# The second layer's last stage of a graph-attention kernel: corrections by ScalarE and DMA, block products in another order

## The chip, the cores and the metric

The kernel runs on one core of a Trainium2 chip. The core has TensorE (PE, with its weight loads as PEld), VectorE (DVE), ScalarE (ACT), GpSimd (POOL) and SyncE (SP). Each engine works through a queue of its own in order, and semaphores tie the queues together. Transfers are issued from SP, ACT or POOL and run on 16 shared DMA engines. The metric is the device time of one execution in microseconds; lower is better.

## The reference

Two layers of graph attention on 512 nodes with 768 features, with 16,896 edges, a residual and a layer norm:

```python
def gat_layer(x, W, a_s, a_d, b, edge_index, concat):
    h = (x @ W).reshape(n, H, C)
    alpha_s = jnp.einsum('nhc,hc->nh', h, a_s)
    alpha_d = jnp.einsum('nhc,hc->nh', h, a_d)
    e = jax.nn.leaky_relu(alpha_s[src] + alpha_d[dst], NEG_SLOPE)
    m = jax.ops.segment_max(e, dst, num_segments=n)
    e = jnp.exp(e - m[dst])
    denom = jax.ops.segment_sum(e, dst, num_segments=n)
    alpha = e / (denom[dst] + EPS)
    out = jax.ops.segment_sum(h[src] * alpha[:, :, None], dst, num_segments=n)
    ...
    return out + b
h = gat_layer(x, W1, a_src1, a_dst1, b1, edge_index, concat=True)    # 8 heads of 768
h = jax.nn.elu(h)
out = gat_layer(h, W2, a_src2, a_dst2, b2, edge_index, concat=True)  # 1 head of 768
x = _layernorm(x + out, axis=-1)
```

## The kernel before

All matrices are float32. The edge list becomes a 512 x 512 matrix of counts, so that the softmax over edges is a dense softmax over rows, and the sum over edges is a dense product. Nodes are held in four tiles of 128 rows, t = 0 to 3, features in six chunks of 128. For each of the 8 heads the kernel projects x, makes the softmax, aggregates and multiplies into the second layer's input h2. Products are made from blocks with fewer multiplications than usual: seven block products (named P1 to P7) take the place of eight, and sums of blocks before and after make up for it.

What each engine does in which order is written out by hand: `run(script, ops)` goes through a string of names and calls the operation behind each. The engines wait for each other by semaphores that follow from the tiles read and written. The last script is `END`. It holds the last head's aggregation (names such as P10), its product with the second weight matrix (m.P1.0 with the eviction e.P1.0), the second layer's softmax (2lift, 2leak, 2rank, 2den, 2part, 2in), and the last stage, which the change is about: the second layer's aggregation, the residual and the layer norm.

In that last stage PT holds the four quadrants of the transposed, unnormalized attention matrix. `2in3` is the last of four copies on ACT (L906) that put the transposed tiles into PT. Sums of quadrants are made on DVE: a0 to a3 on the attention side (L1316, L1317), c0 to c3 on the feature side (L1318, L1319). `f.P6.0` is the block product P6 for the first of two tiles of a half (`final`, two matmuls of 384 columns in the program, four in the trace). Each takes a PSUM bank as accumulator: A for P1 and P2, B for a copy of P1 with P6, P7 and P4 added, F for P5 and P3. `f.fork0` is the copy from bank A into bank B on ACT (`fork_`, L1336); P2 may add to A only after it.

The output is xr + rden * (accumulated products), where xr holds x + b2, row tile by row tile, in an SBUF tile (named hs in the trace, as is the output tile), and rden is the inverse of the softmax denominators. The evictions on DVE are named by quadrant and half: y11 (rows 0 and 1, left 384 columns), y21 (rows 2 and 3, left), y22 (rows 2 and 3, right), y12 (rows 0 and 1, right). They are made by `result` (L1347), which also starts the row's statistics (L1353). The right half needs bank B at two earlier moments as well: after P6 (`xu0`, `xu1` for rows 0 and 1) and after P7 (`xw0`, `xw1` for rows 2 and 3). There `less_` (L1340) computes B * rden - xr into xr on DVE, and the later evictions subtract xr. P7 may add to B only after xu has read it, P4 only after xw, and P3 may add to F only after y22.

At a row's end come the aggregate of its statistics and a square root on ACT (`all`, L1359, L1361), the reciprocal and the offset (`inv`, L1366, L1368), a scaling of the row on ACT and a transfer to the output (`whole`). The row that comes last, row 3, is finished in two halves, on ACT and on DVE (`right3`, `left3`), and its last eviction is cut into pieces of 256 and 128 columns (y21.1a, y21.1b).

Of the kernel before, what the change touches and what calls it, by code (L numbers as in the profile page):

```python
# [8 lines left out]
F32 = mybir.dt.float32  # L9
# [4 lines left out]
AF = mybir.ActivationFunctionType  # L14
ALU = mybir.AluOpType
# [22 lines left out]
def gat_pass(  # L38
# [29 lines left out]
    L, R = slice(0, HALF), slice(HALF, D)  # L68
# [7 lines left out]
    small = ctx.enter_context(tc.tile_pool(name="small", bufs=4))  # L76
# [51 lines left out]
    W1, W2, A, kept_tiles = {}, {}, {}, {}  # L128
# [24 lines left out]
    TH = 2 * P  # L153
# [127 lines left out]
    for j in range(2):  # L281
        nc.vector.tensor_reduce(picks[:, j:j + 1], ident.rearrange("p (j k) -> p k j", k=32)[:, j, :], axis=AX.X,
                                op=ALU.add)
# [30 lines left out]
    else:  # L314
# [808 lines left out]
    def fold(parts):  # L1123
# [22 lines left out]
        """m.P12 lift2 lift3 F2 e.P12 g.P13 m.P1 e.P1 g.P11 m.P0 leak2 e.P0 m.P13 g.P10 rank2 out1 m.P10 e.P13 g.P6 e.P10 in0  # L1146
        m.P4 leak3 rank3 e.P4 m.P11 seed g.P8 w.P3 out2 m.P6 e.P11 g.P3 e.P6 g.P14 m.P8 w.P7 m.P14 e.P14 g.P5 m.P3 out3 l1
        in1 e.P3 m.P7 m.P5 e.P7 l2 l3 e.P5 e.P8"""]
    END = """in2 P10 fork0 ls0 in3 P11 fork1 P20 ls1 P21 P12 n0 nn0 n1 fork2 N0 nn1 r0 P22 n2 nn2 r1 P50 N2 P60 u0 r2 P61 P70 u1
        w0 r3 N1 x0 P71 P40 w1 b0 P30 y0 ls2 B0 vadd P62 P51 u2 P41 x1 b1 P72 w2 P31 y1 B1 P42 f0 P52 f1 F0 x2 m.P1.0 ls3 ld2  # L1150
        b2 B2 P32 e.P1.0 m.P1.1 ld0 y2 F1 f2 ld1 m.P2.0 F2 ld3 e.P1.1 g.0 m.P2.1 rows0 w.0 g.1 rows1 row2 g.3 e.P2.1 m.P6.0
        e.P2.0 spread m.P6.1 own g.2 2lift1 e.P6.0 m.P7.0 m.P7.1 2lift0 w.1 2leak0 2leak1 e.P7.0 2lift2 2rank1 2lift3 fold2
        2leak2 2rank0 m.P4.0 e.P7.1 2rank2 2leak3 2part0 2den0 2den1 m.P4.1 2rank3 fold0 2part1 e.P4.0 e.P4.1 2part2 2in0
        m.P5.0 2part3 e.P6.1 m.P5.1 2den3 fold4 e.P5.0 2den2 2in1 fold1 m.P3.0 e.P5.1 m.P3.1 2in2 e.P3.0 2in3 f.P1.0 f.fork0
        f.P1.1 fold5 fold3 e.P3.1 c0 a0 f.P2.0 c1 a1 a2 y11.0 f.fork1 f.P2.1 c2 y11.1 f.P5.0 f.P6.0 xu0 c3 f.P6.1 xu1 f.P7.0
        a3 xw0 f.P7.1 y22.0 xw1 f.P5.1 f.P3.0 y22.1 f.P3.1 y12.0 f.P4.0 all0 f.P4.1a y12.1 inv0 all1 f.P4.1b whole0 y21.0
        all2 inv1 inv2 y21.1a whole1 whole2 hint y21.1b all3 inv3 right3 left3"""
# [93 lines left out]
    xr = load_x()  # L1251
# [71 lines left out]
    def final(p, i, name, cols=L):  # L1323
        def f():
            start = (name, i) not in bank
            if start:
                bank[name, i] = mm.next()
            for k in range(2):
                nc.tensor.matmul(bank[name, i][:, cols], A2[p][:, k, i * P:(i + 1) * P], C2[p][:, k, cols],  # L1329
                                 start=start and k == 0, stop=k == 1, skip_group_check=True)  # L1330
        return f

    def fork_(i):
        def f():
            bank["B", i] = mm.next()
            nc.scalar.copy(bank["B", i][:, :HALF], bank["A", i][:, :HALF])  # L1336
        return f

    def less_(i, t, cols):
        return lambda: nc.vector.scalar_tensor_tensor(xr[:, t, cols], bank["B", i][:, :HALF], rden[t], xr[:, t, cols],  # L1340
                                                      op0=ALU.mult, op1=ALU.subtract)

    def result(name, i, t, cols, op, free, place=None):
        def f():
            if y[0] is None:
                y[0] = hpool.tile([P, NT, D], F32, name="hs")
            nc.vector.scalar_tensor_tensor(y[0][:, t, cols], bank[name, i][:, cols if cols != R else L], rden[t],  # L1347
                                           xr[:, t, cols], op0=ALU.mult, op1=op)
# [4 lines left out]
            nc.vector.bn_stats(stats[t][:, (0 if cols == L else 1) if place is None else place, :], y[0][:, t, cols])  # L1353
        return f

    def whole_row(t):
        def f():
            mv[t] = small.tile([P, nc.vector.BN_AGGR_DIM], F32, name="mv")
            nc.vector.bn_aggr(mv[t], stats[t])  # L1359
            rstd[t] = small.tile([P, 1], F32, name="rstd")  # L1360
            nc.scalar.activation(rstd[t], mv[t][:, 1:2], AF.Sqrt, bias=eps_ln)  # L1361
        return f

    def inverse(t):
        def f():
            nc.vector.reciprocal(rstd[t], rstd[t])  # L1366
            off[t] = small.tile([P, 1], F32, name="off")
            nc.vector.scalar_tensor_tensor(off[t], mv[t][:, 0:1], -1.0, rstd[t], op0=ALU.mult, op1=ALU.mult)  # L1368
        return f

    def right_out(t):
        def f():
            nc.scalar.activation(y[0][:, t, R], y[0][:, t, R], AF.Identity, bias=off[t], scale=rstd[t])
            nc.scalar.dma_start(out[t * P:(t + 1) * P, R], y[0][:, t, R])
        return f

    def left_out(t):
        def f():
            nc.vector.tensor_scalar(y[0][:, t, L], y[0][:, t, L], mv[t][:, 0:1], rstd[t], op0=ALU.subtract, op1=ALU.mult)
            nc.sync.dma_start(out[t * P:(t + 1) * P, L], y[0][:, t, L])  # L1380
        return f

    for i in range(2):
        for p, name in (("P1", "A"), ("P2", "A"), ("P6", "B"), ("P7", "B"), ("P4", "B"), ("P5", "F"), ("P3", "F")):
            ops[f"f.{p}.{i}"] = final(p, i, name)
        ops.update({f"f.fork{i}": fork_(i), f"xu{i}": less_(i, i, R), f"xw{i}": less_(i, 2 + i, R),
                    f"y11.{i}": result("A", i, i, L, ALU.add, True), f"y21.{i}": result("B", i, 2 + i, L, ALU.add, True),
                    f"y22.{i}": result("F", i, 2 + i, R, ALU.subtract, False),
                    f"y12.{i}": result("F", i, i, R, ALU.subtract, True)})
    def row_out_whole(t):  # L1390
        def f():
            nc.scalar.activation(y[0][:, t, :], y[0][:, t, :], AF.Identity, bias=off[t], scale=rstd[t])
            nc.sync.dma_start(out[t * P:(t + 1) * P, :], y[0][:, t, :])
        return f

    wide_part, last_part = slice(0, TH), slice(TH, HALF)
    for n, part_, place in (("a", wide_part, 0), ("b", last_part, 2)):
        ops[f"f.P4.1{n}"] = final("P4", 1, "B", part_)
        ops[f"y21.1{n}"] = result("B", 1, 3, part_, ALU.add, False, place)
    for t in range(NT):  # L1400
        ops.update({f"all{t}": whole_row(t), f"inv{t}": inverse(t)})
        if t + 1 < NT:
            ops[f"whole{t}"] = row_out_whole(t)
    ops.update(right3=right_out(3), left3=left_out(3))

    def hint():
        if not general:
# [33 lines left out]
```

## Time and profile before

| | us |
|---|---|
| median of 3 runs (616.43 to 617.2) | 616.57 |
| the profiled execution | 617.08 |
| its span | 615.3 |
| PE busy in it | 603.7 (98%) |
| DVE busy | 518.4 (84%) |
| ACT busy | 303.9 (49%) |
| POOL busy | 90.5 (15%) |
| last stage, from the first block product to the last aggregate | 588.28 to 609.16 |

The span runs from the first to the last record of the profiled execution; launch and end lie outside it. Times in the views count from the start of the span. Busy time of PE comes from modelled ends, so a busy PE is not a PE at its peak. The chain of waits follows the last instruction back, at each step to what released it. In the timeline a row gives start, duration, engine, line and tile names, and in brackets how long the engine had been idle before and what released it. A row can stand for several instructions (x4).

### The profile page before, as it was taken

What the parts mean: (1) busy time and instruction counts of PE and PEld (TensorE: products, weight loads), DVE (VectorE), ACT (ScalarE), POOL (GpSimd) and SP (SyncE); (2) the same over time, 40 slices, a digit from 0 to 9 for tenths busy, and PEclk for the clock granted to TensorE, in tenths of its full rate; (3) what the DMA queues carried; (4) which work ended last, traced back from release to release, by engine and by line L of the source; (5) the groups of instructions that cost most, each with busy time, mean ns of one, the idle gap of its engine ahead of it and who ended that gap; (6) DMA issues with size and microseconds to landing.
All of it is one profiled execution on the core that took longest, in us unless ns stands there. A gap on an engine that the chain in (4) does not pass through costs nothing.

```text
span 615.3 us, 8250 instructions
## 1 busy us (share of the span) xinstructions
PE 603.7 (98%) x2777; PEld 487.3 (79%) x2777; DVE 518.4 (84%) x1027; ACT 303.9 (49%) x556; POOL 90.5 (15%) x130
## 2 busy tenths in 40 slices
PE   8999999999999999999999999999999999999994
PEld 5665676688888888888888888888888888886652
DVE  6979967989997789878997789968996799868886
ACT  3118765623746166433746066432746056654643
POOL 1210103031300302022300303022200301020000
PEclk9999999999999999999999999999999999999998
DMA  8973898895947959295956959196875949290122
GB/s 290 312 160 95 242 248 226 224 278 81 342 77 230 214 176 243 52 337 79 334 98 198 234 160 271 37 325 104 292 143 157 271 96 275 42 215 2 32 38 106
DMA packets 95277, 112.85 MB, mean 183 GB/s; under 512 B 42822, under 2 KB 76158, under 8 KB 94334
## 3 DMA queue, kind: packets, MB, share of 16 engines
q1 hardware_dynamic: 74814, 89.06, 46.0%
q0 software_dynamic: 19984, 22.61, 23.1%
q10 hardware_dynamic: 432, 0.59, 0.3%
q8 instruction: 24, 0.39, 0.2%
q14 instruction: 23, 0.19, 0.1%
HBM read 98.73 MB, written 2.90 MB: 165 GB/s over the span
## 4 chain that ended last, share of the span: by engine, by line
PE 96%; DMA 2%; DVE 1%; ACT 1%; issue 0%; SPq 0%; ACTq 0%
PE mm L547 25%; PE mm L470 25%; PE mm L969 23%; PE mm L411 15%; PE mm L1329 2%; DMA hs<-in_x_dram 2%; PE tr L411 1%; PE bc L778 1%; PE mm L655 1%; PE tr L969 1%; DVE st L1353 0%; DVE hs L1347 0%; PE tr L1265 0%; PE mm L298 0%; PE tr L1329 0%; PE bc L1286 0%
## 5 line engine op out<-in xcount | busy, mean ns | idle before, releaser
L476 ACT ACTIVATE hs<-mm 128x512 f32<-128x512 f32 x36 | 21.5, 597 | 113.7 <-PE mm L470 111.1
L478 DVE TENSOR_TENSOR hs<-hs,mm 128x512 f32<-128x512 f32 x54 | 37.1, 687 | 39.9 <-PE mm L470 28.3
L969 PE MATMUL mm<-PT,hs 128*128 128x256 f32 x280 | 66.4, 380 | 1.0 <-ACT mm L975 0.5
L555 DVE TENSOR_TENSOR h<-h,mm 128x512 f32<-128x512 f32 x84 | 57.2, 682 | 7.5 <-PE mm L547 6.6
L969 PEld LDWEIGHTS mm<-PT,hs 128*128 128x128 f32 x280 | 52.8, 190 | 9.1 <-ACT mm L975 1.1
L547 PE MATMUL mm<-w1r,gT 128*128 128x256 f32 x240 | 54.8, 379 | 0.0
L547 PEld LDWEIGHTS mm<-w1r,gT 128*128 128x128 f32 x240 | 45.5, 190 | 6.4 <-DVE h L555 0.2
L187 POOL DMA_DIRECT2D w2t<-in_L_gnn_W_dram x18 | 24.7, 1682 | 143.8 <-DVE h L555 139.6
L470 PE MATMUL mm<-w2r,xT 128*128 128x256 f32 x192 | 44.5, 379 | 0.0
L470 PE MATMUL mm<-w2r,gT 128*128 128x256 f32 x192 | 44.4, 379 | 0.0
L898 ACT ACTIVATE q<-q,rden 128x512 f32<-128x512 f32 x28 | 20.2, 720 | 46.1 <-DVE rden L882 45.8
L906 ACT COPY PT<-zr 128x1024 uint16<-128x1024 uint16 x35 | 40.5, 1158 | 2.7 <-DMA zr<-nr 1.3
L470 PEld LDWEIGHTS mm<-w2r,xT 128*128 128x128 f32 x192 | 36.5, 190 | 5.2
L470 PEld LDWEIGHTS mm<-w2r,gT 128*128 128x128 f32 x192 | 36.5, 190 | 5.0
L695 ACT ACTIVATE q<-q,nmax 128x512 f32<-128x512 f32 x36 | 26.0, 722 | 28.3 <-DVE nmax L692 28.2
L969 PE MATMUL mm<-pS,gS 128*128 128x256 f32 x168 | 39.7, 379 | 0.0
L969 PEld LDWEIGHTS mm<-pS,gS 128*128 128x128 f32 x168 | 31.7, 190 | 4.6
L547 PE MATMUL mm<-w1t,gT 128*128 128x256 f32 x144 | 34.1, 380 | 0.0
L547 PE MATMUL mm<-w1t,gS 128*128 128x256 f32 x144 | 34.0, 379 | 0.0
L187 POOL DMA_DIRECT2D w2r<-in_L_gnn_W_dram x12 | 15.9, 1328 | 122.8 <-PE mm L969 44.2
L470 PE MATMUL mm<-w2t,xS 128*128 128x256 f32 x144 | 33.0, 379 | 0.0
L420 DVE SCALAR_TENSOR_TENSOR scr<-hs,a_s 128x768 bf16<-128x768 f32 x32 | 30.6, 956 | 0.7
(285 smaller groups left out, 1321.0 us busy)
## 6 DMA issues: line engine op xcount, KB each, us to landing
w2r<-in_L_gnn_W_dram SPq DMA_DIRECT2D x48, 384.0 KB
w1r<-in_L_gnn_W_dram SPq DMA_DIRECT2D x43, 384.0 KB
gT<-xd SPq DMA_DIRECT2D x6, 1280.0 KB
w2t<-in_L_gnn_W_dram SPq DMA_DIRECT2D x18, 256.0 KB
w2t<-in_L_gnn_W_dram POOLq DMA_DIRECT2D x18, 256.0 KB, 9.2
w1t<-in_L_gnn_W_dram SPq DMA_DIRECT2D x18, 256.0 KB
w1t<-in_L_gnn_W_dram POOLq DMA_DIRECT2D x18, 256.0 KB, 5.4
a_s<-in_L_gnn_a_src_dram SPq DMA_DIRECT2D x8, 384.0 KB
```

Source lines behind the costliest of these rows:

```text
L187: return lambda: nc.gpsimd.dma_start(o, part(k, n), accum_op=add)
L411: nc.tensor.matmul(ps[:, :HALF], A_[p][:, k, i * P:(i + 1) * P], B_[p][:, k, :], start=start and k == 0, stop=k == HK - 1, skip_group_chec ...
L420: return [lambda al=al, a=a, sign=sign: nc.vector.scalar_tensor_tensor(scr, HS[h][:, t, :], sign, a, op0=ALU.mult, op1=ALU.mult, accum_out ...
L470: nc.tensor.matmul(bank[chain][:, i * TH:(i + 1) * TH], A_[p][:, k, i * P:(i + 1) * P], B_[p][:, k, :], start=first and i == k == 0, stop= ...
L476: nc.scalar.activation(out(o), ps, AF.Copy, scale=how)
L478: nc.vector.tensor_tensor(out(o), out(o), ps, op=how)
L547: nc.tensor.matmul(bank[chain][:, i * TH:(i + 1) * TH], A_[p][:, k, i * P:(i + 1) * P], B_[p][:, k, :], start=first and i == k == 0, stop= ...
L555: nc.vector.tensor_tensor(out(o), out(o), ps, op=how)
L695: nc.scalar.activation(q, q, AF.Exp, bias=nmax, scale=-1.0, accum_out=dens[t])
L898: nc.scalar.activation(q, q, AF.Copy, scale=rden)
L906: copy(PT.rearrange("p s n -> p (s n)").bitcast(U16).rearrange("p (s n h) -> p s n h", s=NT, h=2)[:, :, t * P:(t + 1) * P, :], parted.pop( ...
L969: nc.tensor.matmul(st[bank][:, :HN], A_[p][:, k, c * P:(c + 1) * P], B_[p][:, k, :], start=start and k == 0, stop=k == 1, skip_group_check ...
```

## The change

The change concerns the last script and the operations of the last stage.

- `negative_r`: for each row tile, ACT makes a tile of -rden (names neg0 to neg3).
- `less_` no longer runs on DVE. ACT scales bank B by -rden into a work tile of 384 columns (named zr, from a pool with three buffers), and a DMA issued by POOL adds that tile to the right half of xr in SBUF: 128 rows of 384 floats, 192 KB, four times. The evictions of the right half then add xr, as those of the left half do, and wait for the DMA.
- `result` is only the eviction; the statistics are an operation of their own (`stat`, names s11.0 and so on), which the script places.
- The block products come in another order: P4.0, P3.0, P5.1, P4.1, P3.1 last, with P3.1 cut into two pieces. Row 1 is the row that comes last, finished in two halves, and its right half is the one evicted in pieces (y12.1a, y12.1b).
- Earlier in the script some operations of DVE and ACT change places: the logit sums ls and ld, the operand sums g and w, the lifts, one denominator, two evictions.

```diff
-    END = """in2 P10 fork0 ls0 in3 P11 fork1 P20 ls1 P21 P12 n0 nn0 n1 fork2 N0 nn1 r0 P22 n2 nn2 r1 P50 N2 P60 u0 r2 P61 P70 u1
...
+    END = """ls0 in2 P10 in3 fork0 P11 fork1 P20 ls1 P21 P12 n0 nn0 n1 fork2 N0 nn1 P22 r0 n2 nn2 r1 P50 N2 P60 u0 r2 P61 P70 u1 w0 r3 x0 N1 ...
...
-    def less_(i, t, cols):
-        return lambda: nc.vector.scalar_tensor_tensor(xr[:, t, cols], bank["B", i][:, :HALF], rden[t], xr[:, t, cols],
-                                                      op0=ALU.mult, op1=ALU.subtract)
-
-    def result(name, i, t, cols, op, free, place=None):
+    minus_r = {}
+
+    def negative_r(t):
+        def f():
+            minus_r[t] = small.tile([P, 1], F32, name="mr")
+            nc.scalar.activation(minus_r[t], rden[t], AF.Copy, scale=-1.0)
+        return f
+
+    def less_(i, t):
+        def f():
+            part = work.tile([P, N], F32, name="zr", bufs=3)[:, :HALF]
+            nc.scalar.activation(part, bank["B", i][:, :HALF], AF.Copy, scale=minus_r[t])
+            nc.gpsimd.dma_start(xr[:, t, R], part, accum_op=ALU.add)
+        return f
+
+    def result(name, i, t, cols, free):
         def f():
             if y[0] is None:
                 y[0] = hpool.tile([P, NT, D], F32, name="hs")
-            nc.vector.scalar_tensor_tensor(y[0][:, t, cols], bank[name, i][:, cols if cols != R else L], rden[t],
-                                           xr[:, t, cols], op0=ALU.mult, op1=op)
+            nc.vector.scalar_tensor_tensor(y[0][:, t, cols], bank[name, i][:, :HALF], rden[t],
+                                           xr[:, t, cols], op0=ALU.mult, op1=ALU.add)
             if free:
                 mm.release(bank[name, i])
+        return f
+
+    def part_result(lo, hi):
+        return lambda: nc.vector.scalar_tensor_tensor(
+            y[0][:, 1, HALF + lo:HALF + hi], bank["F", 1][:, lo:hi], rden[1], xr[:, 1, HALF + lo:HALF + hi],
+            op0=ALU.mult, op1=ALU.add)
+
+    def stat(t, cols, place):
+        def f():
             if t not in stats:
-                stats[t] = small.tile([P, 3 if t + 1 == NT else 2, nc.vector.BN_STATS_DIM], F32, name="st")
-            nc.vector.bn_stats(stats[t][:, (0 if cols == L else 1) if place is None else place, :], y[0][:, t, cols])
+                stats[t] = small.tile([P, 3 if t == 1 else 2, nc.vector.BN_STATS_DIM], F32, name="st")
+            nc.vector.bn_stats(stats[t][:, place, :], y[0][:, t, cols])
         return f
```

The order of ACT around the forks, ahead of P2.0. Before, the copies into PT (L906), the two forks (L1336 there), and the table load for the square root:

```order
L906 COPY PT<-zr 128x4x256 x3
L1336 COPY mm_99<-mm_96 128x384
L1336 COPY mm_98<-mm_97 128x384
L1361 ACT_TABLE_LOAD
L1361 ACTIVATE rstd<-mv,eps_ln 128x1 x2
```

Now, with the negations (mr), the forks (L1328) and the four corrections (zr):

```order
L906 COPY PT<-zr 128x4x256 x3
L1336 ACTIVATE mr<-rden 128x1 x2
L1328 COPY mm_99<-mm_96 128x384
L1336 ACTIVATE mr<-rden 128x1 x2
L1328 COPY mm_98<-mm_97 128x384
L1342 ACTIVATE zr<-mm_99,mr 128x384 x2
L1342 ACTIVATE zr<-mm_98,mr 128x384 x2
L1373 ACT_TABLE_LOAD
```

Two negations stand between the last copy and the first fork, two between the forks; the four corrections and their readers are new, and the table load has moved behind them.

The order of PE from P2.0 to the end. A product on xT and pS is P6 or P5, one on h and PT is P2 or P7, one on h and pS is P3, one on xT and PT is P4. Before, from the first P2:

```order
L1329 MATMUL mm_96<-h_631,PT 128x384 x2
L1329 MATMUL mm_97<-h_631,PT 128x384 x2
L1329 MATMUL mm_95<-xT,pS 128x384 x2
L1329 MATMUL mm_99<-xT,pS 128x384 x2
L1329 MATMUL mm_98<-xT,pS 128x384 x2
L1329 MATMUL mm_99<-h_631,PT 128x384 x2
L1329 MATMUL mm_98<-h_631,PT 128x384 x2
L1329 MATMUL tr<-xT,pS 128x384 x2
L1329 MATMUL mm_95<-h_631,pS 128x384 x2
L1329 MATMUL tr<-h_631,pS 128x384 x2
L1329 MATMUL mm_99<-xT,PT 128x384 x2
L1329 MATMUL mm_98<-xT,PT 128x256 x2
```

Now the same stretch:

```order
L1321 MATMUL mm_96<-h_631,PT 128x384 x2
L1321 MATMUL mm_99<-xT,pS 128x384 x2
L1321 MATMUL mm_97<-h_631,PT 128x384 x2
L1321 MATMUL mm_99<-h_631,PT 128x384 x2
L1321 MATMUL mm_98<-xT,pS 128x384 x2
L1321 MATMUL mm_95<-xT,pS 128x384 x2
L1321 MATMUL mm_98<-h_631,PT 128x384 x2
L1321 MATMUL mm_99<-xT,PT 128x384 x2
L1321 MATMUL mm_95<-h_631,pS 128x384 x2
L1321 MATMUL tr<-xT,pS 128x384 x2
L1321 MATMUL mm_98<-xT,PT 128x384 x2
L1321 MATMUL tr<-h_631,pS 128x256 x2
```

P6.0 (mm_99 on xT and pS) has moved ahead of P2.1, P7.0 follows at once, P4.0 (mm_99 on xT and PT) is the tenth product, and P3.1 (tr on h and pS) is the last.

The order of DVE from y22.0 on, the eviction of bank F (mm_95) for row 2. Before, with a correction (L1340) between evictions and each eviction followed by its statistics:

```order
L1347 SCALAR_TENSOR_TENSOR hs<-mm_95,rden,hs 128x384
L1353 BN_STATS st<-hs 128x6
L1340 SCALAR_TENSOR_TENSOR hs<-mm_98,rden,hs 128x384
L1347 SCALAR_TENSOR_TENSOR hs<-tr,rden,hs 128x384
L1353 BN_STATS st<-hs 128x6
L1347 SCALAR_TENSOR_TENSOR hs<-mm_95,rden,hs 128x384
L1353 BN_STATS st<-hs 128x6
L1359 BN_AGGR mv<-st 128x2
L1347 SCALAR_TENSOR_TENSOR hs<-tr,rden,hs 128x384
L1353 BN_STATS st<-hs 128x6
```

Now:

```order
L1350 SCALAR_TENSOR_TENSOR hs<-mm_95,rden,hs 128x384
L1365 BN_STATS st<-hs 128x6
L1350 SCALAR_TENSOR_TENSOR hs<-mm_99,rden,hs 128x384
L1365 BN_STATS st<-hs 128x6
L1371 BN_AGGR mv<-st 128x2
L1350 SCALAR_TENSOR_TENSOR hs<-mm_95,rden,hs 128x384
L1378 RECIPROCAL rstd<-rstd 128x1
L1380 SCALAR_TENSOR_TENSOR off<-mv,rstd 128x1
L1365 BN_STATS st<-hs 128x6
L1350 SCALAR_TENSOR_TENSOR hs<-tr,rden,hs 128x384
```

The corrections are gone from this queue, y21.0 (mm_99) is the second eviction, and row 2 is finished between y12.0 and its statistics. On POOL, where nothing stood behind the four additions of b2 to xr, four rows of L1343 are new.

More of the change, by code (lines that the diff above doesn't have):

```diff
@@ L1385, in gat_pass @@
             ops[f"f.{p}.{i}"] = final(p, i, name)
[L1386 to L1389, printed above, removed]
+        ops.update({f"f.fork{i}": fork_(i), f"xu{i}": less_(i, i), f"xw{i}": less_(i, 2 + i)})
+        for n, name, t, cols, free in (("11", "A", i, L, True), ("21", "B", 2 + i, L, True), ("22", "F", 2 + i, R, False),
+                                       ("12", "F", i, R, True)):
+            ops[f"y{n}.{i}"] = result(name, i, t, cols, free)
+            ops[f"s{n}.{i}"] = stat(t, cols, 0 if cols == L else 1)
     def row_out_whole(t):
@@ L1394, in row_out_whole @@
         return f
[L1396 to L1399, printed above, removed]
+    for n, lo, hi, place in (("a", 0, TH, 1), ("b", TH, HALF, 2)):
+        cols = slice(HALF + lo, HALF + hi)
+        ops[f"f.P3.1{n}"] = final("P3", 1, "F", slice(lo, hi))
+        ops[f"y12.1{n}"] = part_result(lo, hi)
+        ops[f"s12.1{n}"] = stat(1, cols, place)
     for t in range(NT):
-        ops.update({f"all{t}": whole_row(t), f"inv{t}": inverse(t)})
-        if t + 1 < NT:
+        ops.update({f"all{t}": whole_row(t), f"inv{t}": inverse(t), f"neg{t}": negative_r(t)})
+        if t != 1:
             ops[f"whole{t}"] = row_out_whole(t)
-    ops.update(right3=right_out(3), left3=left_out(3))
+    ops.update(right1=right_out(1), left1=left_out(1))
     def hint():
```

9 lines of the change are left out of this document (1 added, 8 removed).

## The prediction

> **What bounds the kernel now.** I read the page's totals and chain first, then the chain in order of time from 588 us, then the timeline of the last 25 us engine by engine, and last the transfers that POOL issues.
>
> ```profile
> PE 96%; DMA 2%; DVE 1%; ACT 1%; issue 0%; SPq 0%; ACTq 0%
> ```
>
> TensorE carries 96% of the chain, so until the last product only what stops PE costs time. The profiled execution took 617.08 us with its span of 615.3 and the 1.8 around it, 0.51 above the median of 616.57; my sum is a difference against this execution and is then applied to the median. The chain in order of time (start, us, what):
>
> ```profile
> 588.28 11.84 PE mm L1329 x36
> 600.12 1.29 PE tr L1329 x4
> 601.41 1.30 PE mm L1329 x4
> ...
> 610.15 0.71 ACT hs L1373
> ```
>
> The last stage has 14 block products of 1.29 us. Nine of them take 11.84 instead of 9 x 1.29 = 11.63, so 0.21 is lost somewhere; the tenth ends at 601.41. From there the chain is on DVE and ends on ACT. The timeline of DVE (start, us):
>
> ```profile
> 596.29 0.62 DVE L1340 SCALAR_TENSOR_TENSOR hs<-mm,rden,hs 128x384 f32<-128x384 f32 x1
> 596.83 0.95 DVE L1319 TENSOR_TENSOR xT<-xT,h 128x768 f32<-128x768 f32 x1
> ...
> 601.45 0.62 DVE L1347 SCALAR_TENSOR_TENSOR hs<-tr,rden,hs 128x384 f32<-128x384 f32 x1 [0.20 <-PE tr L1329]
> 602.10 0.56 DVE L1353 BATCH_NORM_STATS2 st<-hs 128x6 f32<-128x384 f32 x1
> ...
> 603.39 0.56 DVE L1353 BATCH_NORM_STATS2 st<-hs 128x6 f32<-128x384 f32 x1
> 603.99 0.21 DVE L1359 BATCH_NORM_AGGREGATE mv<-st 128x2 f32<-128x12 f32 x1
> 604.11 0.56 DVE L1347 SCALAR_TENSOR_TENSOR hs<-tr,rden,hs 128x384 f32<-128x384 f32 x1
> 604.71 0.56 DVE L1353 BATCH_NORM_STATS2 st<-hs 128x6 f32<-128x384 f32 x1
> 605.19 0.15 DVE L1366 RECIPROCAL rstd<-rstd 128x1 f32<-128x1 f32 x1
> 605.37 0.16 DVE L1368 SCALAR_TENSOR_TENSOR off<-mv,rstd 128x1 f32<-128x1 f32 x1
> 605.45 0.20 DVE L1359 BATCH_NORM_AGGREGATE mv<-st 128x2 f32<-128x12 f32 x1
> ...
> 607.61 0.48 DVE L1347 SCALAR_TENSOR_TENSOR hs<-mm,rden,hs 128x256 f32<-128x256 f32 x1
> 608.12 0.43 DVE L1353 BATCH_NORM_STATS2 st<-hs 128x6 f32<-128x256 f32 x1
> 608.47 0.33 DVE L1347 SCALAR_TENSOR_TENSOR hs<-mm,rden,hs 128x128 f32<-128x128 f32 x1
> 608.83 0.29 DVE L1353 BATCH_NORM_STATS2 st<-hs 128x6 f32<-128x128 f32 x1
> 609.16 0.24 DVE L1359 BATCH_NORM_AGGREGATE mv<-st 128x2 f32<-128x18 f32 x1
> ```
>
> At 601.45 DVE waits 0.20 for the tenth product; from then to 609.16 it hardly pauses, 7.71 us for five evictions (one in two pieces), their statistics and four row ends. From the distances between starts I take the steps: an eviction 0.65 if the next instruction needs it (601.45 to 602.10), 0.54 if not (596.29 to 596.83); statistics 0.60 and 0.48; an aggregate 0.12 (603.99 to 604.11); a reciprocal with its offset 0.18 + 0.08.
>
> **Head of the script.** Before 588 us only the order changes: logit sums, a denominator and some evictions trade places on DVE, and one lift on ACT. The tightest place I found is the eviction e.P5.0, which frees the bank of m.P3.0:
>
> ```profile
> 583.11 0.55 DVE L509 TENSOR_TENSOR h<-h,mm 128x384 f32<-128x384 f32 x1
> ...
> 583.93 0.51 PEld L411 LDWEIGHTS mm<-w2r,gS 128*128 128x128 f32 x2
> ```
>
> It moves behind a denominator and e.P6.1, about 0.26 later by the same steps, and ends at 583.92, just in front of the load at 583.93. PE's row of work covers all this: 0, with ends of -0.1 and +0.3.
>
> **The four negated reciprocals (negative_r).** They stand on ACT ahead of the forks:
>
> ```profile
> 589.23 1.16 ACT L906 COPY PT<-zr 128x1024 uint16<-128x1024 uint16 x1 [1.34 <-DMA zr<-nr]
> 590.30 1.06 ACT L1336 COPY mm<-mm 128x384 f32<-128x384 f32 x2
> 590.82 2.23 PEld L1329 LDWEIGHTS mm<-h,PT 128*128 128x128 f32 x8 [0.58 <-ACT mm L1336]
> 591.38 1.28 ACT L1361 ACT_TABLE_LOAD   x1
> 591.90 0.69 DVE L1316 TENSOR_TENSOR pS<-pS,PT 128x512 f32<-128x512 f32 x1
> 605.68 0.29 ACT L1361 ACTIVATE rstd<-mv,eps_ln 128x1 f32<-128x1 f32 x1 [1.16 <-DVE mv L1359]
> 605.89 1.01 ACT L1392 ACTIVATE hs<-hs,off,rstd 128x768 f32<-128x768 f32 x1
> ```
>
> P2.0's weight load starts at 590.82 when the first fork, begun at 590.30, ends: that is the lost 0.21. Behind fork0 in ACT's queue nothing is in a hurry, but PE is. A one-column activation takes ACT 0.21 (605.68 to 605.89). Two of them come after the last transposed copy, which waits for its transfer, and before fork0: +0.42 on PE. The other two stand ahead of fork1, whose reader now comes two products later: 0. P6.0 moves up to fourth place and needs the sum that DVE ends at 591.90 + 0.69 = 592.59, while PE would want it at about 592.53: +0.08. In all PE runs 0.50 behind, and the tenth product ends at 601.91. If the negations cost nothing this is 0.08; I take 0.50, since the queue is in order.
>
> **The corrections (less_).** Four DVE instructions go:
>
> ```profile
> L1340 DVE SCALAR_TENSOR_TENSOR hs<-mm,rden,hs 128x384 f32<-128x384 f32 x4 | 2.5, 613 | 0.0
> ```
>
> That is 2.45 us of DVE, all between 596 and 601.3. In the new order DVE waits there: y11.1 for P2.1, y22.0 for P5.0 and a landing, y21.0 for the tenth product. So the time saved becomes idle time, worth 0 at the end. On ACT each correction is a scaled copy, 0.55 as an estimate (one copy of L1336 is about 0.47, from two in 1.06 with a wait between). The table load of 1.28 moves behind them, to about 601.3; the first aggregate comes near 603.4, so ACT's idle time still covers it, with 0.8 to spare.
>
> **The new wait: a transfer between product and eviction.** y22.0 needs the second transfer (xw0), y22.1 the fourth (xw1), and P3.0 needs y22.0 to have emptied its bank. The trace shows SBUF-to-SBUF additions only at three times the size, and the nearest size only from DRAM:
>
> ```profile
> 37.83 0.90 POOL L250 DMA_DIRECT2D w2t<-w2t  x1 [10.59 <-DMA w2t<-in_L_gnn_W_dram]
> ...
> 541.79 0.41 ACT L1001 ACTIVATE nl<-nl 128x256 f32<-128x256 f32 x1
> 542.32 0.90 POOL L1253 DMA_DIRECT2D hs<-in_L_gnn_b_dram  x1 [26.95 <-ACT nl L1001]
> ```
>
> ```profile
> w2t<-w2t POOLq DMA_DIRECT2D x2, 576.0 KB, 5.2
> ...
> DMA to landing us min/median/max: 4.3/7.7/10.8
> ```
>
> Busy time and DMA share in three stretches of L250 (bounds, us, engines, clock, share, GB/s):
>
> ```profile
> 37.83:39.25 1.42, 1.42 (x23) 0.74 (x25) 1.39 (x4) 0.45 (x1) 0.90 (x1) 1.00 0.07 16
> 39.25:42.00 2.75, 2.75 (x90) 2.56 (x80) 0.10 (x3) 0.03 (x1) 0.00 (x0) 1.00 1.10 217
> 42.00:43.03 1.03, 1.03 (x4) 0.63 (x5) 1.00 (x5) 0.00 (x0) 0.00 (x0) 1.00 0.07 9
> ```
>
> 1.42 us pass before data moves, 2.75 while it moves, 1.03 until it counts as landed. For 192 KB a third of the data time gives 1.42 + 0.92 + 1.03 = 3.37. The bounds are 2.45 (no time for data) and 5.2 (no gain from size). The smallest landing of L187's 256 KB is 4.3, with a read from DRAM; I take 3.5, near the scaled row, since that has the same path. P7.0 ends at 601.41 + 0.50 - 4 x 1.29 = 596.75; xw0 0.03 + 0.55, hand-over to POOL 0.12 (542.20 to 542.32), 3.5, wake-up 0.05: y22.0 starts at 601.00 and ends at 601.62, 0.13 before P3.0's first matmul, due at 601.75. The Trainium skill, DMA: Bandwidth & Descriptors, section Anatomy of one DMA, gives about 2.0 us plus bytes over 436 GB/s; that would be 2.45 us here, an estimate, and would end y22.0 at 600.57. The trace disagrees for the size it shows: the same formula makes 3.35 of the 5.2 us.
>
> **The tail, walked.** y22.0 601.00, s22.0 601.65, y21.0 602.13, s21.0 602.78, aggregate 603.38, y12.0 603.50 (P3.0 ended at 603.21), its row end and s12.0 604.30, y22.1 ready at 604.78. xw1 follows the ninth product, end 600.62: landed and seen at 604.87. Then aggregate 605.41, s22.1 605.53, row end 606.01, y21.1 606.27, s21.1 606.92, aggregate 607.52, y12.1a 607.64, row end 608.04, s12.1a 608.30, y12.1b 608.65, s12.1b 609.01, last aggregate 609.34 instead of 609.16: +0.18. What follows is the same for row 1 as it was for row 3. Keeping statistics apart saves about 0.1 per pair; five evictions are left after the tenth product, as before, and that product ends 0.50 later. Sum: 617.08 + 0.18, in the median 616.75, say 616.8.
>
> **Rivals.** First, late landing, on the slower side: SBUF-to-SBUF additions take the 5.2 of L250 whatever their size. DVE is dense from y22.0 on, so each us above 3.5 is a us at the end: +0.18 + 1.7, 618.5. It decides from a landing of 4.55 us, where 0.2% (1.23 us, about what a measurement of this kernel can tell from no change) is passed. For it speaks the 4.3 at 256 KB; against it that data moved during 2.75 of the 5.2.
> Second, full relief: the 2.45 us leave DVE's chain and evictions move up, 614.1. Against it stands 601.45's wait on PE: the products come when they come.
> Third, POOL's descriptors for xw0 (from 597.45) wait until DVE pauses. DVE is on its last operand sum and statistics until about 598.5, so y22.0 is 1.05 later: 617.8; if xw1 pays too, between s22.0 and y21.0, about 618.2. Against it: L250's 0.90 stood beside a DVE busy for 1.39 of 1.42 us. The Trainium skill, SBUF — State Buffer, section Who interferes with whom, has DVE's two-port modes lock GpSimd out of writing descriptors, and says that tensor_tensor has no such mode; by that rule nothing would be blocked here.
>
> **How the numbers follow.** My sum has 0.54, late landing 0.27, full relief 0.11, blocked descriptors 0.08, of which half passes 1.23. So slower 0.31, faster 0.11, same 0.58. The likeliest case alone runs from 616.0 (negations free, early landing) to 617.7. The range takes in the late landing with the head's +0.3: 615.9 to 618.9; full relief stays outside.
>
> **What would show it.** A weight load for P2.0 near 591.24 with a longer wait on ACT; DVE idle before y11.1, y22.0 and y21.0; landings of L1343 near 3.5; y22.0 released by a DMA; last aggregate near 609.3. The prediction is wrong if landings are over 4.5, if POOL's issue grows well past 0.90, or if the tenth product does not end at 601.9.

## The result, and the profile after

The kernel after takes 617.94 us (median of 22 runs, 616.84 to 618.69), the kernel before 616.60 on the same chip (22 runs, 615.64 to 617.32). The ratio is 1.0021 with a 95% interval of 1.0014 to 1.0027: 0.9 to 1.7 us slower, 1.3 in the middle. The forecast was 616.8; the time lies inside the range, but 1.1 us above the sum.

The two profiled executions hide this: 615.3 us of span before, 615.1 after. The first product of the last stage starts at 588.12 before (588.28 in the chain, which counts it from the end of the product ahead of it) and at 586.85 after, and the issue of the transposing transfer that brings its last block stands as far ahead of that in both (2.41 and 2.40 us). So the 1.27 us lie earlier, where two executions of one kernel differ by 0.8 to 0.9 (the second profiles below start this stage at 587.21 and 587.60), and clock times of two profiles can't be set side by side. I count from a mark inside the stage instead: the start of the last transposed copy on ACT (PT<-zr), at 589.23 before and 588.16 after, which waits for a landing that starts ahead of everything new in the last stage. What lies after it splits in two:

| counted in us | before | after | forecast for after |
|---|---|---|---|
| copy to weight load of P2.0 | 1.59 | 1.79 | 2.01 |
| copy to the end of the tenth product | 12.18 | 12.71 | 12.68 |
| copy to y22.0 | (no landing) | 11.61 | 11.77 |
| copy to the last aggregate | 19.93 | 19.95 | 20.11 |
| last aggregate to the last transfer's issue (ACT's queue) | 1.73 | 1.73 | 1.73 |
| that issue to the end of the span | 4.41 | 5.26 | 4.41 |

In these two profiles the stage itself ends 0.02 later. Their difference, 0.85, is in the last row, behind the last instruction of any computing engine. First the stage. The chain of the kernel after, by engine, and in order of time (start, us, what):

```profile
PE 93%; DVE 3%; DMA 1%; ACT 1%; issue 0%; DVEq 0%
...
584.45 3.69 DMA zr<-nr
588.16 1.17 ACT PT L906
...
590.83 0.70 DVE pS L1308
591.53 0.04 issue
591.57 8.02 PE mm L1321 x24
599.59 0.18 issue
599.77 0.63 DVE hs L1350
...
608.11 0.25 DVE mv L1371
...
609.10 0.71 ACT hs L1385
```

Before, TensorE carried the chain through the start of this stage. Now it runs through the transposing transfer, its copy and DVE's operand sum, to P6.0 at 591.57: the product that moved up to fourth place. ACT's timeline at the forks:

```profile
588.16 1.16 ACT L906 COPY PT<-zr 128x1024 uint16<-128x1024 uint16 x1 [1.32 <-DMA zr<-nr]
589.23 0.29 ACT L1336 ACTIVATE mr<-rden 128x1 f32<-128x1 f32 x2
589.42 0.47 ACT L1328 COPY mm<-mm 128x384 f32<-128x384 f32 x1
```

Two negations delay the fork by 0.19, from 589.23 to 589.42. The weight loads of PE that waited:

```profile
589.95 0.94 PEld L1321 LDWEIGHTS mm<-h,PT 128*128 128x128 f32 x4 [0.96 <-ACT mm L1328]
591.57 0.94 PEld L1321 LDWEIGHTS mm<-xT,pS 128*128 128x128 f32 x4 [0.68 <-DVE pS L1308]
```

P2.0 starts at 589.95, so PE could take P6.0 1.29 later, at 591.24, and takes it at 591.57. The fork and this wait, 0.20 and 0.33, make the tenth product 0.53 later. PE's rows of it, before (P5.1, which ends at 601.41) and after (P4.0, which ends at 600.87):

```profile
599.96 1.45 PE L1329 MATMUL tr<-xT,pS 128*128 128x384 f32 x4
```

```profile
599.42 1.45 PE L1321 MATMUL mm<-xT,PT 128*128 128x384 f32 x4
```

DVE then takes back nearly all of it: from the eviction behind the tenth product to the last aggregate it needs 7.20 (600.91 to 608.11) instead of 7.71 (601.45 to 609.16). DVE's timeline:

```profile
594.46 0.62 DVE L1350 SCALAR_TENSOR_TENSOR hs<-mm,rden,hs 128x384 f32<-128x384 f32 x1 [0.83 <-PE mm L1321]
...
599.77 0.62 DVE L1350 SCALAR_TENSOR_TENSOR hs<-mm,rden,hs 128x384 f32<-128x384 f32 x1 [2.30 <-PE mm L1321]
600.42 0.56 DVE L1365 BATCH_NORM_STATS2 st<-hs 128x6 f32<-128x384 f32 x1
600.91 0.62 DVE L1350 SCALAR_TENSOR_TENSOR hs<-mm,rden,hs 128x384 f32<-128x384 f32 x1
...
603.61 0.62 DVE L1350 SCALAR_TENSOR_TENSOR hs<-tr,rden,hs 128x384 f32<-128x384 f32 x1
```

The corrections' time has become idle time ahead of y11.1 (0.83) and y22.0 (2.30). The bracket of y22.0 names PE, but its product P5.0 had ended by 598.29 (P6.1 and P5.0 run for 2.74 from 595.55); what came at 599.7 is xw0's transfer, issued at 596.68 with a landing 3.0 later:

```profile
596.68 0.86 POOL L1343 DMA_DIRECT2D hs<-zr  x1 [1.47 <-ACT zr L1342]
...
DMA to landing us min/median/max: 2.9/3.0/3.0
```

Now the end. Line 33 of the kernel is the conditional that closes the program: every engine compares a flag and branches past the fallback pass. Its rows of PE and SP, before:

```profile
L33 SPq EVENT_SEMAPHORE  x8: 17/17/17, 611.5 to 613.6; - x8
L33 PEldq COMPARE_BRANCH  x1: 3312/3312/3312, 602.2 to 602.2; - x1
```

and after:

```profile
L33 SPq EVENT_SEMAPHORE  x8: 17/17/17, 610.4 to 613.4; - x8
L33 PEldq COMPARE_BRANCH  x1: 4102/4102/4102, 604.3 to 604.3; - x1
```

SP's last wait, the one for the outputs, ends 2.7 us after the last issue before (610.89 to 613.6) and 3.6 after (609.84 to 613.4). PE's compare-and-branch takes 3 to 4 us, and it has moved from 8.7 us ahead of the last issue to 5.5 ahead of it. The traffic in tenths of a microsecond shows what that does. GB/s from 1 us ahead of the last issue to 3 us behind it, before:

```profile
GB/s 338 399 431 400 430 430 307 399 430 430 430 277 144 0 92 230 384 307 445 338 338 338 384 384 369 282 31 128 31 15 0 0 0 0 0 0 0 0 0 0
```

and after, with an instruction queue, q8, that is in this window only now (another, q14, moves three pieces of 8 KB behind the last issue in every profile, before and after, so it can't make the difference):

```profile
GB/s 31 31 440 399 369 276 399 430 399 369 369 307 123 0 174 230 338 323 445 353 307 369 399 384 369 139 143 143 46 61 15 31 31 15 31 31 15 31 0 0
...
q8 instruction: 1, 0.02, 2.2%
```

Before, the outputs are through 2.0 us behind the last issue. After, they move as fast until then, and a thread of 15 to 31 GB/s follows for another 0.8 us. The first guess from this: PE's branch fetches two pieces of code of 16 KB, and the second now meets the outputs.

### The profile page after: what moved, and what is told of

Read it like the earlier page. It is cut to its first block, busy times and chain, and to the rows that moved or that the text cites. A ratio compares the mean times of both kernels' runs of the same rounds, so it can differ in the third digit from the quotient of the medians.

```text
span 615.1 us, 8269 instructions
## 1 busy us (share of the span) xinstructions
PE 603.3 (98%) x2777; PEld 486.6 (79%) x2777; DVE 515.9 (84%) x1023; ACT 306.7 (50%) x564; POOL 94.0 (15%) x134
## 4 chain that ended last, share of the span: by engine, by line
PE 93%; DVE 3%; DMA 1%; ACT 1%; issue 0%; DVEq 0%
PE mm L547 25%; PE mm L470 25%; PE mm L969 23%; PE mm L411 13%; PE mm L1321 1%; PE mm L655 1%; PE bc L778 1%; PE tr L411 1%; DMA zr<-nr 1%; PE mm L298 1%; PE tr L969 1%; PE bc L267 1%; DVE st L1365 1%; DMA zr<-pS 1%; DVE hs L1350 0%
## 5 line engine op out<-in xcount | busy, mean ns | idle before, releaser
L906 ACT COPY PT<-zr 128x1024 uint16<-128x1024 uint16 x35 | 40.6, 1159 | 2.5 <-DMA zr<-nr 1.3
```

The lines of the kernel that those rows point to most:

```text
L906: copy(PT.rearrange("p s n -> p (s n)").bitcast(U16).rearrange("p (s n h) -> p s n h", s=NT, h=2)[:, :, t * P:(t + 1) * P, :], parted.pop( ...
```

## The experiments

Two distances are read in each run: from the copy to the last aggregate, and the end (last issue on ACT's queue to the end of the span). My theory had two parts. The stage is worth next to nothing either way, as forecast; the end is longer because PE reaches its branch late: its last product, P3.1, waits for y22.1, while before the last products waited for nothing late and PE's queue ran ahead. Rivals: POOL's late transfers lengthen the end; or the end is scatter; or the stage's waits are what costs.

### Both kernels a second time

> The kernel before, unchanged, profiled a second time. If the differences belong to the kernel: stage 21.0 to 21.1, end 4.3 to 4.6. If the end is scatter, it may be above 5 here.

> The kernel after, unchanged, profiled a second time. Two distances are read in every run from here on: the stage (first product of the last stage on PE to the start of the last aggregate; 21.04 us before, 21.26 after) and the end (issue of the last transfer on ACT's queue to the end of the span; 4.41 before, 5.26 after). If both differences belong to the kernel, the stage is 21.2 to 21.3 and the end 5.1 to 5.4. If the end is only scatter from one execution to the next, it falls anywhere from 4.3 to 5.3.

Before (616.48 us, one run): stage 19.93 from the copy, end 4.60. After (617.90 us, one run): stage 20.06, end 5.42. The end belongs to the kernel: 4.41 and 4.60 against 5.26 and 5.42, 0.8 apart. The distance from the first product varies with the transposed block's landing (3.5 to 3.7 us from issue in these four), the one from the copy does not.

### PE's branch hinted (e1)

The hint for three engines stays; PE gets its own, two products ahead of the end.

```
+def hint_pe():
+    if not general:
+        tc.mark_branch_hint_location("again", "LikelyTaken", [mybir.EngineType.PE])
+ops["hintpe"] = hint_pe
-... y22.1 all0 f.P4.1 s22.1 ...
+... y22.1 all0 hintpe f.P4.1 s22.1 ...
```

> The kernel after, with a branch hint for PE too, issued on PE ahead of the last two products. Theory: PE reaches its final branch late (17.45 us into the stage instead of 14.07, since its last product waits for a late eviction), its branch then takes 4.10 us instead of 3.31 for two code transfers, and the second of these runs beside the output transfers and delays one of them. With the hint the code comes earlier: branch well under 4 us, end back to 4.4 to 4.6, stage unchanged at 21.26, time 617.1. Rival: the end is longer because POOL still has transfers and its own branch at 600 us: end stays at 5.2, time 617.9. Rival: scatter: end anywhere, time 617.9.

616.69 us (11 runs), ratio to before 1.0005 (0.9996 to 1.0014): no longer told apart from before, and 0.4 less than I had expected. End 4.36, stage 19.95 from the copy. The branch, and the traffic in the same stretch as above:

```profile
L33 PEldq COMPARE_BRANCH  x1: 393/393/393, 604.6 to 604.6; - x1
```

```profile
GB/s 0 0 246 430 338 369 461 399 430 430 276 430 123 82 92 230 369 338 399 338 384 323 415 369 369 251 62 128 15 15 0 0 0 0 0 0 0 0 0 0
```

The branch takes 0.39 instead of 4.10, only one piece of code is still fetched, and the thread behind the outputs is gone. POOL has the same four transfers and the same late branch as after, so it is not the cause.

### The kernel before with a late PE (e3)

```
+def late():
+    with_bank = mm.next()
+    nc.tensor.matmul(with_bank[:2, :2], mv[1], mv[1], start=True, stop=True)
+    mm.release(with_bank)
+ops["late"] = late
-... f.P4.1b whole0 y21.0 ...
+... f.P4.1b whole0 late y21.0 ...
```

> The kernel before, with one 2x2 product added on PE behind its last block product; it reads an aggregate that DVE ends some 17.5 us into the stage, so PE reaches its branch as late as it does in the kernel after, and nothing reads the product. Theory of the late PE branch: stage 21.04 as before, end 5.1 to 5.3 instead of 4.41, time 616.6 + 0.8 = 617.4. Rivals (POOL's late branch, or scatter): POOL is as it was, so end 4.4, time 616.6.

617.51 us (11 runs), ratio 1.0015 (1.0006 to 1.0024); end 5.32, stage 20.04.

```profile
L33 PEldq COMPARE_BRANCH  x1: 3482/3482/3482, 605.3 to 605.3; - x1
```

```profile
GB/s 338 338 431 430 399 533 276 399 430 369 430 246 31 82 123 230 369 323 384 338 384 323 399 369 353 200 159 128 61 15 31 31 15 31 15 31 31 0 0 0
```

Nothing of the change is in this kernel but a PE that is late at its branch, and the thread is there. One tiny product that nobody reads costs 0.9 us by the ratio, and 0.9 in the end (5.32 for 4.41).

### The kernel before with the hint (e8)

```
-... f.P4.0 all0 ...
+... hintpe f.P4.0 all0 ...
```

> The kernel before with the same branch hint for PE. There PE's code transfers end 3.4 us ahead of the last output's issue. Theory (only the meeting of the code with the outputs costs time): nothing to save, end 4.4 to 4.6 as before, time 616.5. Rival (the hint saves time by itself, wherever the branch lies): end 0.8 shorter, 3.6, time 615.7.

616.52 us, ratio 1.0000 (0.9991 to 1.0009); end 4.41. The hint saves nothing where the code comes early. All profiles that bear on the end, in order of the last fetch (packets of the instruction queue q8; times in us from the last issue):

| kernel | PE's branch starts | takes | last code fetch ends | end |
|---|---|---|---|---|
| before with the hint (e8) | -8.7 | 0.39 | -6.2 | 4.41 |
| before | -8.7 | 3.31 | -3.4 | 4.41 |
| before with ACT and DMA corrections (e5, below) | -8.6 | 3.38 | -3.3 | 4.43 |
| before, second profile | -8.7 | 3.39 | -3.2 | 4.60 |
| after with the hint (e1) | -5.5 | 0.39 | -2.4 | 4.36 |
| after, negations early (e4, below) | -5.5 | 3.76 | +0.25 | 4.89 |
| before with a late PE (e3) | -5.2 | 3.48 | +0.45 | 5.32 |
| after | -5.5 | 4.10 | +0.7 | 5.26 |
| after, second profile | -5.6 | 4.39 | +1.6 | 5.42 |

The four other kernels with the hint (e6, e7, e9 and e10 below) have their one fetch through 2.4 to 3.1 us ahead of the last issue, and ends of 4.33 to 4.61. So in these profiles a fetch that ends 2.4 us or more ahead of the last issue costs nothing, and one that ends behind it comes with 0.3 to 1.0 more. That the fetch and the late packets share one DMA engine fits a thread of 15 to 31 GB/s, a tenth or less of what all engines moved, but the records don't name the engine: it was not shown.

### The negations early (e4)

The four negated reciprocals move ahead of the last transposed copy, where ACT waits for the landing.

```
-... e.P3.0 2in3 neg0 neg1 f.P1.0 f.fork0 neg2 ... c1 neg3 a1 ...
+... e.P3.0 neg0 neg1 neg2 neg3 2in3 f.P1.0 f.fork0 ... c1 a1 ...
```

> The kernel after with the four negated reciprocals moved ahead of the last transposed copy, into ACT's idle time there (1.32 us). Distances are counted from the start of that copy, since the landing that it waits for comes 3.2 to 3.7 us after its issue in whatever kernel: weight load of P2.0 at +1.59 before and +1.79 after, of P6.0 at +3.41 after, last aggregate at +19.93 before and +19.95 to +20.06 after. Theory: the negations cost PE 0.20 at P2.0, but P6.0 waits for DVE's operand sum behind it and swallows them: P2.0 back to +1.59, P6.0 still at +3.41, last aggregate unchanged, end still 5.2 to 5.4. Rival (the two waits add, as I reckoned): P6.0 and the last aggregate 0.20 earlier.

P2.0 at +1.59 again, P6.0 at +3.41 still, last aggregate +19.95 (616.43 us, one run). PE's timeline:

```profile
587.02 4.16 PE L1321 MATMUL mm<-h,PT 128*128 128x384 f32 x12
591.44 1.56 PE L1321 MATMUL mm<-xT,pS 128*128 128x384 f32 x4 [0.26 <-DVE pS L1308]
```

The third product, P2.0, now follows so soon that it stands in one row with the first two, and P6.0 waits that much longer: its weight load starts 1.82 behind that of P2.0, 0.53 more than a product's 1.29, where it was 0.33 more after. So DVE's operand sum alone sets P6.0, and the negations cost their 0.19 in a place where it is worth nothing. The end was 4.89, 0.3 under what I expected; its fetch ended 0.25 behind the last issue.

### Room for P6.0 by P2.1 (e7)

With the hint and the early negations, P2.1 goes ahead of P6.0.

```
-a1 f.P2.0 f.fork1 f.P6.0 y11.0 xu0 f.P2.1 c2 a2 f.P7.0
+a1 f.P2.0 f.fork1 f.P2.1 f.P6.0 y11.0 xu0 c2 a2 f.P7.0
```

> The kernel after with the hint for PE, the negations early, and P2.1 ahead of P6.0, so that PE has work while DVE makes the operand sum. Theory: P2.0 at copy +1.59, P2.1 behind it, P6.0 at +4.2 without a wait, and every later product 0.6 earlier than after; DVE is dense from y22.0 on, whose transfer leaves 0.6 earlier too: last aggregate at +19.35, end 4.4, time 616.1. Rival (the tail is bound by something else than the start of its chain): last aggregate at +19.7 or later, time 616.5 or more.

617.15 us (ratio 1.0009, 1.0000 to 1.0018), last aggregate at +20.55: 0.6 later than with the hint alone, where I had expected 0.6 earlier. PE's timeline names the reason:

```profile
593.68 1.45 PE L1321 MATMUL mm<-xT,pS 128*128 128x384 f32 x4
595.86 1.56 PE L1321 MATMUL mm<-h,PT 128*128 128x384 f32 x4 [0.73 <-ACT zr L1342]
```

P7.0 adds to the bank from which xu0 takes its scaled copy. With the two products next to each other PE has to wait for ACT; in the change P2.1 stands between them. The move that made P6.0 wait for its operands is what keeps P7.0 from waiting. It also shows how dense DVE is behind y22.0: that eviction came 0.46 later (12.07 for 11.61 from the copy), the last aggregate 0.60.

### The corrections by ACT and DMA in the order of before (e5)

Only the corrections of the change (less_, negative_r, additions in the evictions), with the negations in ACT's idle time.

```
-... e.P3.0 2in3 f.P1.0 ...
+... e.P3.0 neg0 neg1 neg2 neg3 2in3 f.P1.0 ...
-def less_(i, t, cols): (one scalar_tensor_tensor on DVE)
+def less_(i, t): (a copy on ACT scaled by minus_r[t], and dma_start on gpsimd with accum_op=ALU.add)
```

> The kernel before with its own order of products, and the corrections by ACT and a DMA (negations in ACT's idle time). With the order of before the transfer stands close ahead of its reader: P7.0 ends 10.7 us into the stage, the landing is 0.7 + 2.95 later at 14.4, and P3.0, due at 13.3, has to wait for y22.0 until 15.1. Theory: PE loses 1.8 us there, DVE catches up part of it with the 2.45 us of corrections saved, last aggregate 0 to 0.6 later; PE reaches its branch late as well, since its last wait moves back, so the end is 5.0 to 5.4: 617.5 to 618.0. Rival (the order does nothing for the transfer): no wait at P3.0, time as before or less.

620.11 us (4 runs), ratio 1.0064 (1.0048 to 1.0079); last aggregate at +23.15 instead of +19.93, end 4.43. The direction was right and the size far off. ACT's, DVE's and PE's timelines, one row each:

```profile
599.65 0.58 ACT L1350 ACTIVATE zr<-mm,mr 128x384 f32<-128x384 f32 x1 [1.11 <-DMA hs<-zr]
```

```profile
602.36 0.62 DVE L1358 SCALAR_TENSOR_TENSOR hs<-mm,rden,hs 128x384 f32<-128x384 f32 x1 [5.64 <-issue]
```

```profile
603.03 1.56 PE L1329 MATMUL mm<-h,pS 128*128 128x384 f32 x4 [2.60 <-DVE hs L1358]
```

Products of row blocks follow each other there, so the four transfers go out within some 4 us, 6.2 in the kernel after (POOL issues at 596.50, 597.54, 598.83 and 600.52). xw0's, the third, lands 3.5 after its issue instead of 3.0, and the fourth copy waits 1.11 for one of the three buffers to be read. PE stands 2.60 ahead of P3.0, and DVE idles 5.64. So the order of the products is what makes the transfers affordable; the corrections by DMA alone lose 3.6 us. The end, 4.43, was not the 5.0 to 5.4 that I expected: PE's branch is 3.3 us later from the copy than before, but the last issue is 3.2 later too, so the code still comes well ahead of it.

### The corrections back on DVE in the new order (e6)

The other half: after with the hint, less_ as before, no negations, no transfers, and the four corrections placed where DVE idles.

```
-f.P6.0 y11.0 xu0 f.P2.1 c2 a2 f.P7.0 xw0 f.P6.1 y11.1 xu1 s11.0 f.P5.0 c3 a3 f.P7.1 xw1 s11.1 f.P4.0 y22.0 s22.0
+f.P6.0 y11.0 f.P2.1 c2 a2 xu0 f.P7.0 f.P6.1 y11.1 s11.0 xw0 f.P5.0 c3 xu1 a3 f.P7.1 f.P4.0 y22.0 s22.0 s11.1 xw1
```

> The kernel after with the hint for PE (the run with the hint alone had 616.69 us), and the corrections back on DVE, without negations and transfers; on DVE they stand where it idles. Theory: DVE has room for all four, y22.0 no longer waits for a landing, and y21.0 starts when the tenth product ends, 0.2 earlier: last aggregate at copy +19.75 instead of +19.95, end 4.4, time 616.5. Rival (the 2.45 us of DVE that the change saves are worth something at the end): last aggregate 0.3 or more later, time 617 or more.

616.56 us (ratio 1.0001, 0.9992 to 1.0010), last aggregate at +19.84, end 4.33. DVE's row of y21.0:

```profile
601.85 0.62 DVE L1339 SCALAR_TENSOR_TENSOR hs<-mm,rden,hs 128x384 f32<-128x384 f32 x1 [0.39 <-PE mm L1321]
```

With all four corrections back on it, DVE still waits 0.39 for the tenth product, and y21.0 starts 12.75 from the copy, as after (I had expected it 0.2 earlier). The 2.45 us are worth nothing at the end. The stage is even 0.11 shorter, which is no more than the two profiles of the kernel after differ (19.95 and 20.06); the rows put it at y22.1, which no longer waits for the fourth landing and starts 0.47 behind the statistics ahead of it instead of 0.58.

### Each transfer in two (e10)

The hint alone, with each 192 KB addition as two of 96 KB.

```
-nc.gpsimd.dma_start(xr[:, t, R], part, accum_op=ALU.add)
+for j in range(2):
+    c = slice(j * HALF // 2, (j + 1) * HALF // 2)
+    nc.gpsimd.dma_start(xr[:, t, R][:, c], part[:, c], accum_op=ALU.add)
```

> The run with the hint alone, with each correction's transfer split into two of 96 KB, one behind the other on POOL. If the landing has a fixed part and one that goes with the size, as I scaled it from 576 KB, a 96 KB transfer lands in 2.4 to 2.7 us instead of 2.9 to 3.0, and the second of a pair, issued 0.9 later, sets y22.0: 0.3 to 0.6 later than with one transfer, and the last aggregate as much. If the landing hardly goes with the size, each lands in 2.9 to 3.0 and y22.0 is 0.9 later.

```profile
DMA to landing us min/median/max: 2.5/2.9/3.4
```

```profile
601.47 0.62 DVE L1352 SCALAR_TENSOR_TENSOR hs<-mm,rden,hs 128x384 f32<-128x384 f32 x1 [2.76 <-DMA hs<-zr]
```

The time is 618.07 us (one run). The shortest landing, of a half with nothing in front of it, is 2.5; y22.0 starts 12.08 from the copy, 0.47 later than with one transfer, and the last aggregate is 0.53 later (+20.48). Both are what a size term gives. With 96 KB in 2.5, 192 KB in 2.9 to 3.0 and 576 KB in 5.2 a fixed 2.0 us and about 200 GB/s, an estimate from these three, come within 0.3 of each (2.5, 3.0, 4.9). The Trainium skill, DMA: Bandwidth & Descriptors, section Anatomy of one DMA, has the same 2.0 with 436 GB/s; the fixed part agrees, the rate for these additions inside SBUF does not.

### A version from what was learned (e9)

Corrections on DVE, the hint, and a head of the stage in which nothing keeps PE waiting (the edit against e6; y22.0 and its statistics also stand ahead of P4.0 in the script):

```
-e.P3.0 2in3 f.P1.0 f.fork0 f.P1.1 ... c0 a0 c1 a1
-f.P2.0 f.fork1 f.P6.0 y11.0 f.P2.1 c2 a2 xu0 f.P7.0 f.P6.1 y11.1 s11.0 xw0 f.P5.0 c3 xu1 a3 f.P7.1
+e.P3.0 f.P1.0 f.fork0 2in3 f.P1.1 ... c0 c1 a0 a1
+f.P2.0 f.fork1 f.P2.1 f.P6.0 y11.0 c2 a2 f.P6.1 y11.1 xu0 s11.0 f.P7.0 xu1 c3 f.P5.0 xw0 a3 f.P7.1
```

> The run with the corrections on DVE and the hint, and the head of the stage in another order: fork0 on ACT ahead of the last transposed copy instead of behind its landing, P2.1, P6.0 and P6.1 in places 4 to 6, P5.0 between P7.0 and P7.1, so that neither the fork, nor the operand sum, nor a correction keeps PE waiting. Theory: ten products of 1.29 without a gap end 12.9 us into the stage (13.9 with the corrections on DVE alone), y21.0 starts at 12.95 instead of 14.08, and the dense chain from there to the last aggregate takes 7.1 as it did: stage 20.0 instead of 21.2, end 4.4, time 615.4. Rival (DVE has no room for the earlier work): stage 20.6 or more, time 616 or more.

615.56 us (11 runs), ratio to before 0.9982 (0.9973 to 0.9991): 1.0 us faster than before and, by the two ratios, 2.4 faster than after. Its PE and DVE timelines:

```profile
587.85 5.32 PE L1321 MATMUL mm<-h,PT 128*128 128x384 f32 x16
593.01 2.74 PE L1321 MATMUL mm<-xT,pS 128*128 128x384 f32 x8
```

```profile
600.96 0.62 DVE L1339 SCALAR_TENSOR_TENSOR hs<-mm,rden,hs 128x384 f32<-128x384 f32 x1 [0.39 <-PE mm L1321]
...
608.05 0.24 DVE L1360 BATCH_NORM_AGGREGATE mv<-st 128x2 f32<-128x18 f32 x1
```

The fifth product starts at 593.01, 5.16 behind the first, which is four times 1.29: no gap. y21.0 starts 13.11 us into the stage (expected 12.95). From the first product to the last aggregate it is 20.20 us (608.05 - 587.85), for 21.04 before and 21.26 after; from y21.0 on DVE needs 7.09, as expected.

## Why the prediction came out as it did

- **The case** held as far as it went: no large relief, no late landing. Between same and slower it is a near thing, 1.3 us against the 1.23 (0.2%) at which the prediction drew the line. **The range** held by luck: 617.94 is inside 615.9 to 618.9, but beyond the 617.7 to which the likeliest case alone was to run. The room above was meant for a late landing, which did not come, and what filled it was not in the prediction. The sum of +0.18 is 1.1 us short of the measured +1.3.
- **The step that failed** is one sentence of the tail: "What follows is the same for row 1 as it was for row 3." For ACT and DVE it is (1.73 us from aggregate to issue in both), but the end of the program is not only that row. It grew from 4.41 and 4.60 to 5.26 and 5.42, because the order of products put a wait on DVE into PE's last product, and PE's unhinted branch then fetched code beside the outputs. A hint takes that back (e1), a late product alone brings it (e3). The rows of line 33 were in the profile of before: PE's branch took 3.31 us there, and its last fetch, through 3.4 us ahead of the last issue, had no other traffic beside it. I asked which engine waits for whom, and not what each engine does when its queue is empty.
- **Head of the script, 0**: nothing speaks against it. The last transposing issue stands 2.41 and 2.40 ahead of the first product, and over all thirteen profiles that product starts at 587.62 on average, in the five with the old head as in the eight with the new.
- **Negations, +0.42, and P6.0, +0.08**: the total was right, 0.53 at the end of the tenth product for 0.50, and the parts were not. Two negations cost 0.19, because I took the step of 0.21 for each from a square root that also reads a bias column. The Trainium skill, ScalarE: Activation LUTs, section What ACT_TABLE_LOAD costs, gives 186 ns for an activation with immediate scale and bias and an overlap of 93 between two, which makes an estimate of 0.19 for a pair: the trace agrees (589.23 to 589.42). P6.0 waits 0.33, and 0.53 without them (e4). The total came out because DVE's operand sum sets P6.0 whatever the negations cost, up to their 0.42. So the prediction's "If the negations cost nothing this is 0.08" is wrong: P6.0 would then have been due 0.42 sooner and would have waited 0.50. The lower end of the likeliest case, 616.0, counted on that gain. A slip beside it changes nothing: 9 x 1.29 is 11.61, so the fork cost 0.23 before, not 0.21.
- **Corrections, worth 0**: right. DVE idles before y11.1 and y22.0 (not before y21.0), and putting all four back costs nothing (e6). The scaled copy is 0.58 (estimated 0.55), and ACT still has 0.85 in hand at the table load (0.8).
- **Landing, 3.5**: 2.9 to 3.0, below the 3.37 scaled from 576 KB. The estimate of 2.45 by the Trainium skill, DMA: Bandwidth & Descriptors, section Anatomy of one DMA, was too short. The hand-over from ACT to POOL, taken as 0.12, is 0.29 (596.39 to 596.68). Together y22.0 is 0.16 earlier than reckoned.
- **Tail, last aggregate +0.18**: +0.02 and +0.13 from the copy in two profiles. The walk from y21.0 was right, 7.20 for 7.21; what is left is the 0.16 of y22.0.
- **Rivals**: full relief fell with the idle time. Blocked descriptors fell too: POOL's issue is 0.86 beside a busy DVE. Late landing fell as well: no landing of 192 KB was over 3.5, in e5, against the 5.2 of the rival. What it said of the price holds: in the order of before, where the landing is needed sooner, PE stands 2.60 ahead of P3.0.
- **What the sum leaves open**: the end accounts for about 0.8 of the 1.3 us in profiles, and the hint for some 1.0 in times (1.0021 to 1.0005). The remaining 0.3 lies inside the interval of the run with the hint; it may be the 0.02 to 0.13 of the stage and a longer transposed landing, 3.58 on average in seven profiles with the new head for 3.40 in five with the old. The two sets overlap (3.39 to 3.75 and 3.19 to 3.56), so I can't tell it from scatter.

## What to carry to other kernels

Measure a tail in two pieces, to the last issue and from there to the end of the span, and look in the second at what every engine's sequencer does, the idle ones too: an engine whose last wait moves back takes its branch and its code fetch along, into the outputs. Give each engine a hint ahead of its last work, or keep the order such that the engine is through early. Time freed on an engine counts only where that engine is not already waiting; here 2.45 us of DVE were worth nothing, and a better order of the same work, with the hint and no transfer at all, was worth 1.0.

## What was not expected of the hardware

- PE's compare-and-branch takes 3.3 to 4.4 us without a hint and 0.39 with one; on ACT, DVE and SP, which have a hint, it takes 0.07 to 0.09, on POOL, which has none, 0.05. Behind it stand two fetches of 16 KB of 0.9 to 1.7 us each. With the hint one of them remains.
- One 16 KB fetch beside two output transfers of 192 KB moves the last output's end from 2.0 to as much as 3.2 us behind its issue.
- The transposing transfer's landing varied from 3.2 to 3.75 us in the twelve profiles in which the copy on ACT waits for it, and took the products of the stage with it.
